# Score rows and turned states by way of DRAM in a four-layer graph network: one kernel, one change

## The chip, the cores and the metric

The kernel runs on one core of a Trainium2 chip. A core has TensorE (PE) for matrix products, VectorE (DVE), ScalarE (ACT) and GpSimd (POOL) for elementwise work, SyncE (SP), which here only issues transfers, and 16 DMA engines. Matrix products end in PSUM, eight banks of 128 x 512 float32; everything else lives in SBUF (128 partitions) or in DRAM. Each engine works through its own instructions in order and waits for others by semaphores.

The metric is the device time of one execution in microseconds, as the median of three runs: 2783.21 us before the change (2779.62 to 2784.21). About 0.2% (5.6 us) can be told from no change.

## The reference

There are 128 graphs of 128 nodes with 256 features and an adjacency matrix. Four layers follow one another, each with a residual and a normalisation:

```python
x = layernorm(x + L0(x, adj))   # attention, 4 heads of 64
x = layernorm(x + L1(x, adj))   # 3 steps of a gated recurrent unit (GRU)
x = layernorm(x + L2(x, adj))   # relations: one masked sum and product each
x = layernorm(x + L3(x, adj))   # attention, 1 head
```

In an attention layer the score of a pair of nodes is the sum of a row term and a column term:

```python
e = leaky_relu(e_src[:, :, None, :] + e_dst[:, None, :, :], 0.2)
e = where(adj > 0, e, -inf);  alpha = softmax(e, axis=2)
out = elu(einsum('bijh,bjhf->bihf', alpha, Wh))
```

The second term has to lie along the row of the score matrix, the same on all 128 partitions: a column that a product left across partitions must be turned into a row and repeated. In the GRU layer each of three steps does this:

```python
m = h @ weight[i];  aggr = A^T @ m
gi = aggr @ w_ih.T + b_ih;  gh = h @ w_hh.T + b_hh
r = sigmoid(i_r + h_r);  z = sigmoid(i_z + h_z)
n = tanh(i_n + r * h_n);  h = (1 - z) * n + z * h
```

## The kernel before

**Groups and stages.** The graphs go in 33 groups: one of two graphs, 31 of four, one of two. For each group there are stages, written as Python generators; each `yield` ends one step of a stage. The stages are `loads` (l), `head` (h, layer 0), `tail` (t, layers 2 and 3), two lanes of gate products `reset_and_new` and `new_and_update` (p and q), and two lanes for the elementwise part of the GRU, `chunk_0` and `chunk_1` (u and v), one for each half of the 256 features.

**The written order.** Strings of letters say which stage of which group takes its next step. START fills the pipeline, STEPS is one turn of a loop in steady state (31 turns, one for each group of four), END drains it. In a turn, different groups are in different stages. A last pass ties all instructions of an engine to the order in which they were written, so an engine never overtakes: what stands behind a waiting instruction waits too. All transfers of the steady state go through SP's one queue.

**Gates** (L585). The 256 x 256 products of the GRU use Strassen's scheme: seven products instead of eight for each gate and source, with sums of blocks formed by POOL (state) and DVE (aggregate) in `right_sums` (L553, operation at L560). A gate holds a pair of PSUM banks, "sums" (chunk 0) and "gate" (chunk 1), until ACT and DVE have read it. ACT copies at L607 and L609 and DVE additions at L617 and L625 stand between its products (L597). `GATES, OTHERS = 2, 4`: two such pairs, and four banks in turn for everything else ("ps").

**A GRU step** (`chunk`, L637). For each half, ACT makes r, n and z, DVE makes the new state `hT` (L669, L670), features along partitions. For the next step the state is also needed with nodes along partitions: four PE transposes into a ps bank (L679), copied by ACT to `hN` (L683). Then `neighbours` (L571) multiplies it by the adjacency, ACT copies the aggregate (L580), and DVE forms its block sums.

**Score rows** (`as_rows`, L404). DVE splits the column terms into three bf16 parts, which together hold the float32 value (L412 to L415); PE transposes them (L419), ACT copies the rows out (L422). A matmul with a column of ones at the three right places (`picks`) then repeats a row over all partitions (L478 in the head, L800 in the tail), and DVE adds the other term and the mask out of PSUM (L482, L803), giving `em`.

**By way of DRAM.** Four other transpositions already use no PE: `to_dram` (L300) stores a tile, `from_dram` and `squares` (L310, L130) read it back with four DMAs that put 32 x 32 squares in each other's places, and DVE transposes inside the squares (L333, L519, L719, L823). For the first or last group (`by_pe`) PE does it instead.

Of the kernel before, what the change touches and what calls it, by code (L numbers as in the profile page):

```python
# [16 lines left out]
P = 128  # L17
N = 128
# [7 lines left out]
GATES, OTHERS = 2, 4  # L26
# [20 lines left out]
IN_TURN = [("p", 14), ("q", 10), ("u", 3), ("v", 3), ("p", 10), ("q", 14), ("u", 11), ("v", 13)]  # L47
# [4 lines left out]
FIRST = {"a": ("c", 0), "b": ("h", 0), "c": ("l", 0), "d": ("f", 0), "e": ("l", 1), "f": ("h", 1), "g": ("l", 2), "h": ("u", 0), "i": ("v", 0), "j": ("p", 0), "k": ("q", 0), "l": ("h", 2), "m": ("u", 1), "n": ("v", 1), "o": ("t", 0), "p": ("p", 1), "q": ("q", 1)}  # L52
START = """
aaababababcbbbbbcbdbbabbedbbbbdddbdddddddddddddddbbdaabbfddddbbbbbbbbbbbdbbbbbefdddddfbdbbbdbcbddbbd
ddbdffbbbbbffffbdffbcgghfiiijhhhkifijjjjfkjjjfijffjakkkjjkjhfkkkjijjfjjjkheijjjjkkkfkkkkkijkhffffhkk
kfhihhhkhfkhhjiiijkffiiiihfffklhhiijjiikkkijjjjjkjajllkkkjjjkiffflijjhkjhkfjjjkkkffjjjkkkkkhkhhjiihk
khhfffikfiihfliihhhhfjfiihfkkklffffkkiiijjiijjjjjjjkfkkjkfhjjjkaiiljjjkkkjjjkjjlhkhjkkhjdfkkgffhhikk
kikfmnkhliimmhmiiolppplddddpdnnpnqdddddddddddddd
"""
PERIOD = {"a": ("q", 0), "b": ("v", 0), "c": ("t", -2), "d": ("p", 0), "e": ("h", 1), "f": ("u", 0), "g": ("t", -1), "h": ("t", -3), "i": ("l", 2), "j": ("l", -1), "k": ("l", 0), "l": ("h", 2), "m": ("u", 1), "n": ("p", 1), "o": ("v", 1), "p": ("q", 1), "q": ("t", 0)}  # L60
STEPS = """
abcaddddaeaebdedfeedaedaaedabeabfbddfgaacdddeaaddgdafafedhaaeacdgfageaggfbabcaaefficfddbbggaggajeeea
fgggfgfebfgggggggdebbbkaadbblcdbgibbdddacdadacccgdlggcladeeedeelafdebgdbggadaafccccedacdadaaafaddbac
dafdeaffadebafffbdeefegbbdalbfeegefgabbgebfafdbbbeddgaadcbdddeedggeebddaaaefddefbaagbbgddaaeacdadafg
daadiaaaddfdaaaffedgfgllblbfgabbllemmlgnnmggogoonmnbponq
"""
LAST = {"a": ("q", -1), "b": ("l", -2), "c": ("p", -1), "d": ("v", -1), "e": ("t", -3), "f": ("t", -2), "g": ("u", -1), "h": ("t", -4), "i": ("l", -1), "j": ("t", -1)}
END = """
abacaaacaaddacceccfcgccedcahcdcgdccaccaaaaagcaaafggfeefcgaaagffggceefffffeffggaffagddddfffccgddgadcc
ddfaacdafadfcefccaaadffccadfffecaccgcdcggcdaaccccdaaaccgcggaaaaacaaddagdadggggdecaagdfcaafgdaagddcdf  # L70
dccffcdccdeeecfffcfcecfcfaaacfffaeidgdcaeffcgaaacccaafcjaaccgdggagccafjadddafgeaaigddfejjejjjjejjjjj
jjjjffffjjjjjjjffffjjjfffjjjjfjjjjffjjjjjfjjjfffjjjjjjjjjjjjjjjjjjjjjjj
# [8 lines left out]
def kernel(ctx: ExitStack, tc: tile.TileContext, a: dict, out: bass.AP):  # L81
# [88 lines left out]
    def state(g):  # L170
        by_pe = {"head": g == 0, "tail": g == NG - 1}
        return {"g": g, "graphs": spans[g], "n": sizes[g], "relations": 1, "by_pe": by_pe, **layers()}
# [15 lines left out]
    for l, tag in enumerate(("x3T_0", "o", "x3_0")):  # L188
# [34 lines left out]
    identb = cp.tile([P, P], BF16, tag="identb", name="identb")  # L223
    picks = {}
# [4 lines left out]
    def constants(st):  # L229
# [11 lines left out]

        nc.vector.tensor_copy(identb, ident)
        yield
        for T in (G * H, G):
            one = ring(sp, [3 * T, T], F32, "pick", f"one_{T}", 2)
            nc.vector.tensor_add(one, ident[: 3 * T, :T], ident[: 3 * T, T : 2 * T])
            nc.vector.tensor_add(one, one, ident[: 3 * T, 2 * T : 3 * T])
            picks[T] = cp.tile([3 * T, T], BF16, tag=f"pick{T}", name=f"pick_{T}")
            nc.vector.tensor_copy(picks[T], one)
            yield  # L250
# [153 lines left out]
    def as_rows(st, cols, name):  # L404

        n, h = cols.shape[1], cols.shape[2]
        full = ring(sp, [P, 3, G, h], BF16, "split", f"split_{name}", 2)
        if n < G:
            nc.vector.memset(full, 0.0)
        t = full[:, :, :n]  # L410
        r = ring(sp, [P, n, h], F32, "rest", f"rest_{name}", 2)
        nc.vector.tensor_copy(t[:, 0], cols)  # L412
        nc.vector.tensor_sub(r, cols, t[:, 0])
        nc.vector.tensor_copy(t[:, 1], r)
        nc.vector.tensor_sub(t[:, 2], r, t[:, 1])  # L415
        yield
        k = 3 * G * h
        ps = ring(pp, [P, 1024], BF16, "ps", "psb", OTHERS)[:k, :N]
        nc.tensor.transpose(ps, full.rearrange("p k g h -> p (k g h)"), identb)  # L419
        yield  # L420
        st["rows"] = ring(sp, [k, N], BF16, "rows", f"rows_{name}", 2)
        nc.scalar.copy(st["rows"], ps)  # L422
        yield
# [7 lines left out]
    def head(st):  # L431
# [20 lines left out]
        wh = sp.tile([P, n, D + 2 * H], F32, tag="wh0", name=f"wh0_{g0}")  # L452
        for g in range(G):
            if g < n:
                ps = bank(D + 2 * H)
                for c in range(C):
                    matmul(ps, xT[:, c, ts(g, N)], w0[:, c, :], start=c == 0, stop=c == C - 1)
            yield
            if g < n:
                nc.scalar.copy(wh[:, g, :], ps)  # L460
            yield
# [477 lines left out]
```

## Time and profile before

| | us |
|---|---|
| median of three runs | 2783.21 |
| span of the profiled execution | 2778.8 |
| idle time of PE before 138 us | 31.6 |
| idle time of PE after 2622 us | 35.5 |
| one turn of the loop in steady state | 82.8 |

The runs take 0.8 to 5.4 us more than the span, which counts from the first to the last instruction of the profiled execution; no other time of that execution is given. The profile tells busy time by engine, the chain of work that ended last, groups of instructions by source line, and transfers. A product in float32 is recorded as two instructions; a transpose as one. PE's pieces in the chain give the pace at which it moves on, which is shorter than the duration of one instruction, because instructions overlap.

In the table of groups each row has the line, the engine, the operation, what it writes and reads, how often, and then the busy time, the mean of one in nanoseconds, and the idle time before it with what ended that. Four rows for an idea of sizes:

```profile
L580 ACT COPY agT<-ps 128x512 f32<-128x512 f32 (+1 forms) x198 | 112.6, 569 | 100.0 <-PE ps L115 100.0
L482 DVE SCALAR_TENSOR_TENSOR em<-ps,wh,nbias 128x128 f32<-128x128 f32 x512 | 140.6, 339 | 37.3 <-PE ps L115 37.3
L669 DVE SCALAR_TENSOR_TENSOR d<-z,d 128x512 f32<-128x512 f32 (+1 forms) x198 | 147.1, 743 | 15.0 <-ACT h2N L683 10.3
L607 ACT COPY sums<-gate 128x256 f32<-128x256 f32 (+1 forms) x396 | 141.6, 358 | 140.6 <-PE gate L597 138.1
```

### The profile page before, as it was taken

The page shows a single profiled execution, that of the slowest core. Times are in us where ns is not written, and L with a number is a line of the kernel's source. Part 1 is how long each engine was busy: PE and PEld are TensorE (multiplying, and loading weights), DVE is VectorE, ACT ScalarE, POOL GpSimd, SP SyncE. Part 2 cuts the span into 40 slices and gives each one's busy share as a digit, 9 for nine tenths or more (in the row PEclk, how much of TensorE's full clock was granted, in tenths as well). Part 3 has the DMA queues.
Part 4 walks back from the last instruction along what each step waited for, and adds up shares of the span by engine and source line. Part 5 has one row for each costly group of instructions (what it writes and reads, how often), then busy time and mean ns, then how long its engine had stood idle before and what let it go on. Part 6 is the DMA issues. An engine that isn't in the chain of part 4 may idle for free.

```text
span 2778.8 us, 44698 instructions
## 1 busy us (share of the span) xinstructions
PE 2702.2 (97%) x14490; PEld 2293.2 (83%) x14490; DVE 2208.4 (79%) x5269; ACT 1781.0 (64%) x4570; POOL 913.2 (33%) x925
## 2 busy tenths in 40 slices
PE   6899999999999999999999999999999999999986
PEld 4788888888888888888888888888888888888874
DVE  6677887878888878888877888887888787888765
ACT  3556766666666666666666666666766666666645
POOL 0223333324333323333323333323333333333331
PEclk9999999999999999999999999999999999999997
DMA  3344455444555444545444545445446545445321
GB/s 101 68 83 95 90 112 111 86 93 92 108 102 113 85 92 97 108 96 118 89 88 98 103 95 118 95 88 97 98 95 118 101 88 100 93 97 107 80 51 47
DMA packets 1177038, 263.73 MB, mean 95 GB/s; under 512 B 929888, under 2 KB 1176544, under 8 KB 1176800
## 3 DMA queue, kind: packets, MB, share of 16 engines
q1 hardware_dynamic: 1172272, 257.00, 46.0%
q10 hardware_dynamic: 4528, 3.81, 0.5%
q8 instruction: 118, 1.93, 0.3%
q14 instruction: 120, 0.98, 0.1%
HBM read 153.10 MB, written 107.61 MB: 94 GB/s over the span
## 4 chain that ended last, share of the span: by engine, by line
PE 93%; DVE 4%; ACT 1%; DMA 1%; issue 0%; POOL 0%; SPq 0%; ACTq 0%; POOLq 0%; DVEq 0%
PE gate L597 44%; PE ps L115 29%; PE sums L597 18%; PE ps L118 2%; DVE em L482 1%; DVE gate L625 1%; ACT em L397 0%; PE psb L419 0%; DMA vec<-in_L_gnn_a_dst_dram 0%; DMA factors_h<-in_L_gnn_w_hh_dram 0%; DVE d L669 0%; DVE em L393 0%; DVE nm L394 0%; DVE sums L617 0%; DVE st_x L347 0%
## 5 line engine op out<-in xcount | busy, mean ns | idle before, releaser
L597 PE MATMUL gate<-T_h,factors_h 128*128 128x256 f32 (+1 forms) x2376 | 691.5, 379 | 10.1 <-DVE gate L625 8.6
L597 PE MATMUL gate<-T_a,factors 128*128 128x256 f32 (+1 forms) x2376 | 677.3, 373 | 2.2 <-DVE T_a L560 2.0
L597 PEld LDWEIGHTS gate<-T_h,factors_h 128*128 128x128 f32 x2376 | 424.5, 190 | 93.3 <-DVE gate L625 27.6
L597 PEld LDWEIGHTS gate<-T_a,factors 128*128 128x128 f32 x2376 | 443.9, 191 | 59.2 <-DVE T_a L560 2.5
L597 PE MATMUL sums<-agT,factors 128*128 128x256 f32 (+1 forms) x1188 | 347.5, 374 | 2.2 <-ACT sums L607 1.0
L661 ACT ACTIVATE n<-n,bih 128x512 f32<-128x512 f32 (+1 forms) x198 | 140.5, 709 | 264.7 <-DVE n L659 264.7
L397 ACT ACTIVATE em<-em,nm 128x128 f32<-128x128 f32 x640 | 247.9, 391 | 6.3 <-DVE nm L394 6.2
L597 PEld LDWEIGHTS sums<-agT,factors 128*128 128x128 f32 x1188 | 220.5, 190 | 35.9 <-DVE sums L617 1.6
L664 POOL TENSOR_TENSOR d<-h2T,n 128x512 f32<-128x512 f32 (+1 forms) x66 | 82.2, 1245 | 466.9 <-ACT n L661 466.9
L607 ACT COPY sums<-gate 128x256 f32<-128x256 f32 (+1 forms) x396 | 141.6, 358 | 140.6 <-PE gate L597 138.1
L722 POOL TENSOR_TENSOR x<-x,x 128x512 f32<-128x512 f32 x63 | 78.8, 1272 | 458.2 <-DVE x L719 444.7
L360 ACT ACTIVATE x<-x,mr_x,rs_x 128x256 f32<-128x256 f32 x384 | 198.7, 589 | 11.2 <-DVE mr_x L355 11.2
L115 PE MATMUL ps<-wh,aT 128*128 128x64 f32 (+1 forms) x1280 | 188.5, 295 | 1.3 <-PE gate L597 0.6
L597 PE MATMUL gate<-agT,factors 128*128 128x256 f32 (+1 forms) x594 | 178.6, 382 | 2.4 <-ACT r L649 2.4
L115 PEld LDWEIGHTS ps<-wh,aT 128*128 128x128 f32 x1280 | 169.1, 192 | 12.9 <-PE gate L597 1.5
L580 ACT COPY agT<-ps 128x512 f32<-128x512 f32 (+1 forms) x198 | 112.6, 569 | 100.0 <-PE ps L115 100.0
L353 POOL TENSOR_TENSOR rs_x<-rs_x,neghalf 128x4 f32<-128x4 f32 (+1 forms) x99 | 98.8, 998 | 232.1 <-DVE rs_x L352 232.1
L657 DVE SCALAR_TENSOR_TENSOR n<-r,n 128x512 f32<-128x512 f32 (+1 forms) x198 | 127.0, 668 | 58.0 <-ACT n L655 58.0
L482 DVE SCALAR_TENSOR_TENSOR em<-ps,wh,nbias 128x128 f32<-128x128 f32 x512 | 140.6, 339 | 37.3 <-PE ps L115 37.3
L669 DVE SCALAR_TENSOR_TENSOR d<-z,d 128x512 f32<-128x512 f32 (+1 forms) x198 | 147.1, 743 | 15.0 <-ACT h2N L683 10.3
L353 POOL TENSOR_TENSOR rs_o<-rs_o,neghalf 128x4 f32<-128x4 f32 (+1 forms) x33 | 43.4, 1314 | 349.9 <-DVE rs_o L352 343.7
L752 POOL TENSOR_TENSOR x<-x,b 128x256 f32<-128x256 f32 x128 | 133.1, 1068 | 52.2 <-ACT h1N L683 45.0
(170 smaller groups left out, 6123.0 us busy)
## 6 DMA issues: line engine op xcount, KB each, us to landing
d_em<-em SPq DMA_DIRECT2D x63, 512.0 KB, 3.4
aT<-d_em SPq DMA_DIRECT2D x252, 128.0 KB, 3.7
x0s<-in_x_dram SPq DMA_DIRECT2D x248, 64.0 KB, 2.6
adj<-in_adj_dram SPq DMA_DIRECT2D x62, 256.0 KB, 3.3
x<-in_x_dram SPq DMA_DIRECT2D x31, 512.0 KB, 4.8
d_h0T<-x SPq DMA_DIRECT2D x62, 256.0 KB, 3.0
h0T<-d_h0T SPq DMA_DIRECT2D x124, 128.0 KB, 3.8
d_h<-h3T SPq DMA_DIRECT2D x62, 256.0 KB, 2.3
```

The costliest lines, as they stand in the source:

```text
L115: nc.tensor.matmul(ps, lhsT, rhs, start=start, stop=stop)
L353: nc.gpsimd.tensor_tensor(rs, rs, neghalf[:, :n], ALU.pow)
L360: nc.scalar.activation(y[:, g, :], y[:, g, :], AF.Identity, bias=mr[:, g : g + 1], scale=rs[:, g : g + 1])
L397: nc.scalar.activation(em[:, r, :], em[:, r, :], AF.Exp, bias=nm[:, i : i + 1], accum_out=den[:, i : i + 1])
L482: nc.vector.scalar_tensor_tensor(em[:, g - k, h, :], rows_of[g][:, h, :], wh[:, g, D + h : D + h + 1], nbias[:, g, :], ALU.add, ALU.add,)
L580: nc.scalar.copy(t, ps)
L597: nc.tensor.matmul(into, w[:, SEL[name], k - 1], layer[source][k], start=start, stop=True, skip_group_check=True)
L607: nc.scalar.copy(c11, c21)
L657: nc.vector.scalar_tensor_tensor(n, tr, 1.0, n, ALU.add, ALU.mult)
L661: nc.scalar.activation(n, n, AF.Tanh, bias=bih[:, 2 * C + c : 2 * C + c + 1])
L669: nc.vector.scalar_tensor_tensor(d, tz, 1.0, d, ALU.add, ALU.mult)
L752: nc.gpsimd.tensor_add(x2[:, g, :], x2[:, g, :], b2)
```

## The change

Four things change together.

1. Score rows: `as_rows` and the constants `identb` and `picks` go. Each graph's column terms (in the tail: all graphs' at once) are stored to DRAM as rows, one float at a time, by `to_rows`, and read back by `from_rows` with the row repeated over all partitions, straight into `em`. DVE then adds the other term and the mask in place.
2. New states: for all groups but the first and the last (`gru` in `by_pe`) the state `hT` is stored to DRAM as it is, read back in four DMAs of squares into `hN`, and transposed inside the squares by DVE.
3. PSUM: three pairs of gate banks and two other banks.
4. START, STEPS and END are written anew. The loop runs 29 turns; START and END hold the rest. In a turn, steps of the next group's GRU and those of the present one's last step stand side by side. The tile `o` gets a second buffer, DRAM tiles get rings of their own, and `x1` and `edge` are looked up when they are used.

```diff
-GATES, OTHERS = 2, 4
+GATES, OTHERS = 3, 2
...
-PERIOD = {"a": ("q", 0), "b": ("v", 0), "c": ("t", -2), "d": ("p", 0), "e": ("h", 1), "f": ("u", 0), "g": ("t", -1), "h": ("t", -3), "i": ("l", 2), "j": ("l", -1), "k": ("l", 0), "l": ("h", 2), "m": ("u", 1), "n": ("p", 1), "o": ("v", 1), "p": ("q", 1), "q": ("t", 0)}
+PERIOD = {"a": ("v", -1), "b": ("p", 0), "c": ("q", 0), "d": ("h", 1), "e": ("v", 0), "f": ("u", 0), "g": ("t", -1), "h": ("t", -2), "i": ("l", 2), "j": ("l", -1), "k": ("h", 2), "l": ("t", -3), "m": ("u", 1), "n": ("v", 1), "o": ("p", 1)}
 STEPS = """
...
+abcbcbccdecbfcccghbbcbfcebgcdhcbebibfbeccdgbcbccdcfgjcbcfbdfgceegcighfehdcfcehggbgcfghfccgedeegfbgde
+gdgkccglgdfdcegffcgjcefgebcbehcbdgedcbbdebgbhcbghlhcgcchdbfbdgcbcgbdehbbbhfkcckdbdbcfcbebfbbcfbgdfe
+ecegfdcfbdkgdeecfgcekeggddbdefecggdecgcgdckgdfgccdcfckdgfcdcdbfebhebecdelbgcbcbbcgcibdgebbhcbcdcdbfk
+emmkbblbkbbgkfnbfmcbfbcenbmfbofeefknncooeeocfkoeonoog
 """
...
-        by_pe = {"head": g == 0, "tail": g == NG - 1}
+        by_pe = {"head": g == 0, "gru": g in (0, NG - 1), "tail": g == NG - 1}
...
-    def as_rows(st, cols, name):
...
+    def to_rows(cols, name):
+
+        d = ring(dp, [cols.shape[1], N], F32, "rows", f"d_rows_{name}", 10)
+        nc.sync.dma_start(d.rearrange("r m -> m r"), cols)
+        return d
+
+    def from_rows(t, rows):
+
+        nc.sync.dma_start(t, rows.rearrange("r m -> (r m)").partition_broadcast(P))
...
@@ head
                 nc.scalar.copy(wh[:, g, :], ps)
-            yield
-        yield from as_rows(st, wh[:, :, D + H :], f"0_{g0}")
-        rows = st["rows"]
+                rows[g] = to_rows(wh[:, g, D + H :], f"0_{g0}_{g}")
+            yield
...
             for g in range(k, k + 2):
-                ps = rows_of[g] = bank(H, N)
-                for h in range(H):
-                    i = g * H + h
-                    matmul(ps[:, h, :], picks[G * H][:, i : i + 1].to_broadcast([3 * G * H, P]), rows)
-                yield
+                from_rows(em[:, g - k].rearrange("p h m -> p (h m)"), rows[g])
+            yield
             for g in range(k, k + 2):
                 for h in range(H):
                     nc.vector.scalar_tensor_tensor(
                         em[:, g - k, h, :],
-                        rows_of[g][:, h, :],
+                        em[:, g - k, h, :],
...
@@ chunk
             if l + 1 < L:
 
-                ps = bank(G, N)
-                for g in range(G):
-                    transpose(ps[:, g, :], hT[:, ts(g, N)])
+                by_pe = st["by_pe"]["gru"]
+                if not by_pe:
+                    d = ring(dp, [G * P, P], F32, "turnh", f"d_h{l + 1}{c}_{g0}", 4)
+                    nc.sync.dma_start(d.rearrange("(g p) m -> p g m", p=P), hT.rearrange("p (g m) -> p g m", g=G))
                 yield
                 yield from right_sums(nc.gpsimd, hT, st["layers"][l + 1]["h"], c, f"h{l + 1}_{g0}")
                 hN = ring(sp, [P, G, N], F32, "hN", f"h{l + 1}N{c}_{g0}", 2)
-                nc.scalar.copy(hN, ps)
-                yield
-                yield from neighbours(hN, edge, st["layers"][l + 1]["a"], c, f"{l + 1}_{g0}")
+                flat = hN.rearrange("p g m -> p (g m)")
+                if by_pe:
+                    ps = bank(G, N)
+                    for g in range(G):
+                        transpose(ps[:, g, :], hT[:, ts(g, N)])
+                else:
+                    from_dram(flat, d)
+                yield
+                if by_pe:
+                    nc.scalar.copy(hN, ps)
+                else:
+                    nc.vector.transpose(flat, flat)
+                yield
+                yield from neighbours(hN, st["edge"], st["layers"][l + 1]["a"], c, f"{l + 1}_{g0}")
...
@@ tail
-        yield from as_rows(st, wh[:, :, D + 1 :], f"3_{g0}")
+        rows = to_rows(wh[:, :, D + 1], f"3_{g0}")
+        yield
...
-        ps = bank(n, N)
-        for g in range(n):
-            matmul(ps[:, g, :], picks[G][:, g : g + 1].to_broadcast([3 * G, P]), st["rows"])
+        from_rows(em.rearrange("p g m -> p (g m)"), rows)
...
-    for p in range(1, NG - 1):
+    for p in range(2, NG - 2):
```

## The prediction

> **What bounds the kernel now.** I read the page's busy shares first, then one turn of the loop (82.8 us, four graphs) by stretches, then the chain of waits inside that turn, then the queues.
>
> ```profile
> PE 2702.2 (97%) x14490; PEld 2293.2 (83%) x14490; DVE 2208.4 (79%) x5269; ACT 1781.0 (64%) x4570; POOL 913.2 (33%) x925
> ...
> PE 93%; DVE 4%; ACT 1%; DMA 1%; issue 0%; POOL 0%; SPq 0%; ACTq 0%; POOLq 0%; DVEq 0%
> ```
>
> ```profile
> 1048.30:1131.10 82.80, 82.64 (x445) 70.54 (x444) 68.02 (x161) 55.05 (x141) 28.52 (x28) 1.00 0.49 99
> ```
>
> The single row is the stretch of one turn: length, then busy PE, PEld, DVE, ACT, POOL, granted clock, DMA share. TensorE is full, at clock 1.00, and the chain runs through it for 93%. Busy PE is pipelined, so I price PE work by the chain, whose pieces are the pace at which PE moves on. These pieces of the same turn (start, length, what) are those the change touches:
>
> ```profile
> 1054.91 0.44 PE ps L118 x4
> ...
> 1077.54 0.44 PE ps L118 x4
> ...
> 1081.47 0.44 PE ps L118 x4
> ...
> 1100.96 0.15 PE psb L419
> ...
> 1112.33 0.17 PE psb L419
> ...
> 1113.56 0.55 PE ps L115 x8
> ...
> 1115.20 0.43 DVE gate L625
> 1115.64 1.02 DVE em L482 x4
> 1116.66 0.35 DVE gate L625
> ...
> 1124.47 0.33 PE ps L115 x4
> ...
> 1128.48 0.33 PE ps L115 x4
> 1128.81 0.59 PE ps L118 x4
> ```
>
> L118 are the transposes of new states, L419 the transposed scores, the short L115 pieces the rows laid out by matmul. The DVE pieces are the only real stop of PE in the turn, 1.80 us: L625 stands behind the score additions.
>
> **What goes.** Transposes 0.44+0.44+0.44+0.59 = 1.91 us. Head rows 0.55+0.33+0.33 = 1.21; the tail's four row matmuls start at 1103.02 and PE goes on at 1103.34, so 0.32. L419: 0.15+0.17 = 0.32. Together 3.76 us per turn, all on the path. ACT loses four copies to hN (595 ns) and two to rows (256): 2.9 us, off the path. DVE loses eight split operations of about 0.17 us, 1.4. A floor for a turn without any stop is 82.8 - 3.76 - 1.8 = 77.2 us. Removing the constants (identb, picks) touches only the start, where PE waits for weights; I cost it at nothing.
>
> **What comes, per turn.**
> DVE: four transposes 128x512, the L823 row's 690 ns: 2.8 us. The score additions read SBUF instead of PSUM; L659 has 684 and 672 ns from PSUM where L669 and L670 have 690 to 770 from SBUF, so no change. DVE: 68.0 - 1.4 + 2.8 = 69.4 us. In a turn of 79 that is 88%, against 82% now: not the bound, but each wait of DVE for a transfer now reaches the gate additions (L617, L625) behind it sooner.
>
> SP, which issues everything in order: four stores of states, 16 reads, five stores of score columns, five broadcasts, 30 DMAs beside 49. The reads of d_h take 0.56 us each on SP, stores 0.38 to 0.47: 9.0 + 1.7 + about 4.5 = 15 us, onto 34 us of issues in SP's timeline of this turn. 49 of 79 us: it fits, but each read also waits at the queue's head for its store to land.
>
> DMA engines: 0.487 x 82.8 x 16 = 645 engine-us for 37,254 packets, 17.3 ns each. Added packets: 2048 of 512 B, 8192 of 128 B, 2560 of one float, 640 of 2 KB: 13,440, at the same mean 233 engine-us. (645+233)/16 = 55 us, 69% of 79. Not the bound.
>
> **The new wait: hT by way of DRAM.** Now a turned state costs 0.44 us PE and 0.6 us ACT. Then:
>
> ```profile
> d_h<-h3T SPq DMA_DIRECT2D x62, 256.0 KB, 2.3
> ...
> aT<-d_em SPq DMA_DIRECT2D x124, 64.0 KB, 2.7
> ```
>
> The store has the size of the first row (2.3 us to landing; the like d_h0T takes 3.0). Each of the four reads has the size of the second; the last is issued 1.7 us after the first (0.56 each). With the transpose: 2.3 to 3.1 + 1.7 + 2.7 + 0.69 = 7.4 to 8.2 us from state to edge product. What hides it is PE work written in between. I set each step's instructions beside its letter in the new STEPS and added the PE steps at the pace of the chain (0.43 us for a gate product, 0.88 for an edge product, 1.73 for a w2 pair). Between the state's step and its edge product stand 9.6 and 7.3 us (chunks 0 and 1, first layer) and 9.6 and 8.7 (second layer). On SP chunk 0's reads are written behind chunk 1's store, so they wait for chunk 1's state: 0.4 + 1.7 + 2.7 + 0.69 = 5.5 us, against 5.6 and 5.7 written. So only chunk 1 of the first layer is short, by 0.1 to 0.9 us; I take 0.5. If the cover were gone, each turned state would cost 6.4 to 7.2 us more than now.
>
> **Score rows.** The broadcasts' nearest row is the 256 KB adj load, 3.3 us. A column store writes single floats to DRAM, which no row shows. By number of packets it equals a load of adjacency squares (512 packets, 2.4 to 4.1 us). Against it speaks the Trainium skill, "DMA: Bandwidth & Descriptors": Rules for kernel authors say a strided last dimension becomes one descriptor per element and should be avoided; its Specifications say that below 512 B the engine reads, modifies and writes. If those writes ran one after another at the 0.2 us HBM access of its Latency section, 32 per engine make 6.4 us. The tail's store is written 5.7 us of PE before the additions that use it: by the row 2.6 + 3.3 = 5.9, short by 0.2; by the rule 9.7, short by 4.0 in each turn. Nothing here runs such a write; I take the row, since packets cost 17.3 ns whatever their size, and keep 0 to 4.0. The head's first two columns have 17 us and more of cover; its broadcast is written 3.0 us ahead of its addition, so DVE may wait 0.3 us, which PE need not see.
>
> **Three gate pairs, two other banks.** PE now refills a ps bank after two uses, not four. By the same count the emptying copy or addition is written 0.4 to 1.7 us ahead of the refill in ten places and level with it in one; copies take 0.37 to 0.84. I put 0.8 us per turn on it, 0 to 2. The third gate pair lets r, nh and z of the next layer start sooner: that is the cover above, not a further gain. The DVE stop of 1.8 us: L482 stays, its matmuls go; I leave 0.6. Stops after: 0.5 + 0.2 + 0.8 + 0.6 = 2.1 us.
>
> A second rule against the change: "VectorE: DVE Perf Modes", Rules for kernel authors, has a 128x128 transpose go to TensorE where PSUM will do. By the chain it costs the full engine 0.11 us each; by DVE, an engine with 14.8 us free, 0.17. By the rule the 1.91 us stay and the gain is 59 us smaller; I take the row, because here TensorE sets the turn.
>
> **The sum.** A turn: 77.2 + 2.1 = 79.3, 3.5 less. Over 31 full groups 109 us. The ends (before 138 us and after 2622 us PE is idle 31.6 + 35.5 us by the stretches) are written anew; I leave their idle time, 20 us either way. The span 2778.8 lies 4.4 below the median 2783.2; the difference is taken off the median: **2674 us**.
>
> **Rivals.**
> Covered, as forecast: 0.60, 2615 to 2735 (stops 0.8 to 4.0, ends 20).
> Partly covered: stops of 4 to 5.4, since landings stretch when 30 more DMAs share the queue: about 2755; 0.11. For: the DMA share is up to nine tenths in slices of the turn. Against: the written distances.
> Slower: **SP's single queue makes the turn of states the bound.** The reads of d_h landed in up to 4.7 us. If stores and reads both do so, the chain is 4.7 + 1.7 + 4.7 + 0.69 = 11.8, short by 4.5 in the first layer and 3.1 in the second: stops 7.6 + 1.6 = 9.2, a turn of 86.4, 2895 us. It decides from a chain of 10.0 us on (2 x 10.0 - 7.3 - 8.7 = 4.0, with 1.6 the 5.6 that go). For: DVE at 88% and SP both serve in order. Against: medians of 2.3 to 3.3. Chance 0.25; slow single-float writes end here too.
> Better: no stop but 0.5 us and shorter ends, about 2610; 0.04.
> A measurement tells about 0.2%, 5.6 us, from no change. Faster 0.71, same 0.04 (the edge of the partly covered case), slower 0.25. The range leaves out most of the slower case: 2605 to 2815.
>
> **What would show it.** Right: a turn near 79 us, PE still over 90% of the chain, hN transposes waiting under 1 us for DMA, DVE near 69 us, DMA share near 0.69. Wrong: DVE or PE at the head of the chain waiting for hN or em transfers; column stores landing in over 5 us; SP waiting on its own stores; PE waiting for ps evacuations beyond 2 us a turn.

## The result and the profile after

The changed kernel takes 3866.53 us (median of 4 runs, 3865.49 to 3867.05) against 2782.1 us for the old one beside it: 1.390 times as long, with a 95% interval of 1.388 to 1.392. The forecast was 2674 us, and the range to 2815 us does not hold it. The sign was wrong as well.

The head of the page of the kernel after: span, busy time by engine, the granted clock in 40 slices, and SP's queue.

```profile
span 3863.4 us, 44097 instructions
...
PE 2935.0 (76%) x13290; PEld 2449.9 (63%) x13290; DVE 2396.5 (62%) x5118; ACT 1711.7 (44%) x4380; POOL 877.4 (23%) x925
...
PEclk8889898888888888888888898988888888888987
...
q1 hardware_dynamic: 1607312, 364.34, 64.4%
```

PE has 1200 instructions fewer than before (13290 against 14490), as the change says, but is busy 233 us longer (2935.0 against 2702.2), and for 24% of the span it does nothing. The row of the clock says why fewer instructions take longer: 0.8 to 0.9 of full speed in nearly every slice, 0.862 on average, where before it was 0.993. A wait costs twice here: once for the idle time, and again for the slow pace behind it, as a stretch below shows.

One turn is now 117.3 us (703.5 us over six turns between the first loads of `x0s` of a group), against 82.8. The stretch of most of one turn after, with the same columns as in the prediction:

```profile
1904.30:2020.40 116.10, 90.56 (x406) 76.17 (x405) 74.13 (x156) 52.88 (x134) 27.23 (x28) 0.85 0.69 100
```

Before, a turn had 82.64 us of busy PE in it; less the 3.76 us removed that would be 78.9. Here it is 90.56: 11.7 us more, which is the clock, and 25.5 us in which PE is idle. The DMA share of 0.69 is the number that was forecast, but of a longer turn: 0.69 of 116.1 is 80 us of the engines' time, where 0.69 of 79 was 55. The engines are not full, and still have far more to do than was counted.

What DVE and PE wait for, from the page's groups: busy time and mean, then the idle time before the group and what ended it.

```profile
L463 DVE SCALAR_TENSOR_TENSOR em<-em,wh,nbias 128x128 f32<-128x128 f32 x512 | 244.2, 541 | 226.9 <-DMA em<-d_rows 226.8
...
L123 PE MATMUL ps<-edge,h2N 128*128 128x128 f32 x512 | 99.6, 356 | 210.6 <-DVE h2N L676 210.5
```

The score additions (before L482, now L463) wait for the broadcast of the rows, and the edge product for the turned state. Both are DMA chains, so who holds them up? SP's own waits (line, tile and transfer waited for: us in total, times, longest):

```profile
SPq L408 <- DMA d_rows<-wh: 263.9, 36, 10.5
...
SPq L142 <- DMA d_h<-h2T: 239.3, 35, 9.2
```

The broadcast (L408) stands at the head of SP's queue until the store of the column terms has landed, and the reads of squares (L142) until the store of the state has. The second is a plain 256 KB store, whose like landed in 2.3 us before. One stretch of SP's timeline (start, length, line, transfer) shows it:

```profile
1958.60 0.38 SPq L661 DMA_DIRECT2D d_h<-h2T  x1
1960.73 0.38 SPq L403 DMA_DIRECT2D d_rows<-wh  x1
1961.66 0.36 SPq L661 DMA_DIRECT2D d_h<-h2T  x1
1962.11 12.70 SPq L142 DMA_DIRECT2D h2N<-d_h  x8
1974.91 0.98 SPq L403 DMA_DIRECT2D d_rows<-wh  x2
1983.29 0.34 SPq L408 DMA_DIRECT2D em<-d_rows  x1
```

From the first of the eight reads to the last it takes 12.70 us, where 0.56 each make 4.5. The last four are issued only at 1972.91, when the second store of a state has landed, 11 us after its issue. A store of single floats (1960.73) stands between the two state stores. PE in the same stretch:

```profile
1967.09 0.59 PE L578 MATMUL gate<-T_h,factors_h 128*128 128x256 f32 x2
1974.40 2.05 PE L123 MATMUL ps<-edge,h2N 128*128 128x128 f32 x8 [6.72 <-DVE h2N L676]
1976.24 1.06 PE L578 MATMUL gate<-T_h,factors_h 128*128 128x256 f32 x2
1977.10 1.06 PE L578 MATMUL gate<-h2T,factors_h 128*128 128x256 f32 x2
...
1981.77 0.59 PE L578 MATMUL sums<-h2T,factors_h 128*128 128x256 f32 x2
1982.20 0.59 PE L578 MATMUL gate<-T_a,factors 128*128 128x256 f32 x2
```

PE is idle for 6.72 us; behind it, pairs of a gate product start 0.86 us apart, and from 1981.77 on 0.43 apart. That is the clock: the granted clock of the six microseconds from 1974.40 is 0.50, of the six from 1981.77 it is 0.95. The trace agrees with what the Trainium skill, "TensorE: Matmul & The Clock Gate", Part 1, says of a clock that halves after an idle window and comes back only after sustained work; the page gives about 3.4 us for either, and here the slow pace lasted some 6.

The profile alone doesn't decide between two readings: that the stores of single floats are slow and take the rest with them, or that too many transfers in one queue make the states' way through DRAM late (the prediction's slower rival).

### The profile page after: what moved, and what is told of

Same layout as the page of the kernel before. It is cut to its first block, busy times and chain, and to the rows that moved or that the text cites. A ratio compares the mean times of both kernels' runs of the same rounds, so it can differ in the third digit from the quotient of the medians.

```text
span 3863.4 us, 44097 instructions
## 1 busy us (share of the span) xinstructions
PE 2935.0 (76%) x13290; PEld 2449.9 (63%) x13290; DVE 2396.5 (62%) x5118; ACT 1711.7 (44%) x4380; POOL 877.4 (23%) x925
## 3 DMA queue, kind: packets, MB, share of 16 engines
q1 hardware_dynamic: 1607312, 364.34, 64.4%
## 5 line engine op out<-in xcount | busy, mean ns | idle before, releaser
L578 PE MATMUL gate<-T_a,factors 128*128 128x256 f32 (+1 forms) x2376 | 731.4, 398 | 192.2 <-DVE T_a L541 190.7
L578 PE MATMUL gate<-T_h,factors_h 128*128 128x256 f32 (+1 forms) x2376 | 773.0, 415 | 45.5 <-DVE gate L606 34.7
L578 PEld LDWEIGHTS gate<-T_h,factors_h 128*128 128x128 f32 x2376 | 484.9, 215 | 143.3 <-DVE gate L606 33.9
L463 DVE SCALAR_TENSOR_TENSOR em<-em,wh,nbias 128x128 f32<-128x128 f32 x512 | 244.2, 541 | 226.9 <-DMA em<-d_rows 226.8
L578 PE MATMUL sums<-h2T,factors_h 128*128 128x256 f32 (+1 forms) x396 | 135.7, 428 | 207.0 <-DVE sums L598 204.4
L123 PE MATMUL ps<-edge,h2N 128*128 128x128 f32 x512 | 99.6, 356 | 210.6 <-DVE h2N L676 210.5
L123 PEld LDWEIGHTS ps<-edge,h2N 128*128 128x128 f32 x512 | 90.9, 260 | 226.7 <-issue 213.3
L578 PEld LDWEIGHTS sums<-h2T,factors_h 128*128 128x128 f32 x396 | 78.6, 210 | 230.7 <-DVE sums L598 218.0
L123 PE MATMUL ps<-edge,h1N 128*128 128x128 f32 x512 | 119.5, 409 | 132.4 <-issue 112.5
L123 PEld LDWEIGHTS ps<-edge,h1N 128*128 128x128 f32 x512 | 112.4, 313 | 149.5 <-issue 141.5
```

What stands on the lines that cost most here:

```text
L123: nc.tensor.matmul(ps, lhsT, rhs, start=start, stop=stop)
L463: nc.vector.scalar_tensor_tensor(em[:, g - k, h, :], em[:, g - k, h, :], wh[:, g, D + h : D + h + 1], nbias[:, g, :], ALU.add, ALU.add,)
L578: nc.tensor.matmul(into, w[:, SEL[name], k - 1], layer[source][k], start=start, stop=True, skip_group_check=True)
```

## The experiments

Times are given beside the old kernel's on the same chip, which was 2780.8 to 2784.5 us in all of them. "Turn" is worked out as above over six to nine turns. Runs without an interval are single ones; four runs of the last kernel below lie 12 us apart, so differences of that size between single runs say little.

### What makes the rows and states late

**The rows in the order in which they lie in SBUF.** Each partition stores its column terms side by side, 16 bytes in the head's and 8 to 16 in the tail's store.

```diff
-        d = ring(dp, [cols.shape[1], N], F32, "rows", f"d_rows_{name}", 10)
-        nc.sync.dma_start(d.rearrange("r m -> m r"), cols)
+        d = ring(dp, [N, cols.shape[1]], F32, "rows", f"d_rows_{name}", 10)
+        nc.sync.dma_start(d, cols)
...
-        rows = to_rows(wh[:, :, D + 1], f"3_{g0}")
+        rows = to_rows(wh[:, n - 1, D + 2 - n :], f"3_{g0}")
```

> The changed kernel, but the score columns are stored as they lie: each partition writes its four floats side by side (128 pieces of 16 B), and the broadcast reads the same 2 KB; the tail stores four neighbouring columns of one graph. The scores so laid out are permuted, so values differ from the reference's. Theory A (each store of single floats holds the DMA engines for about 8 us, and all that is queued behind it comes late): about 2700 us, 2640 to 2780. Theory B (turning the states by way of DRAM through SP's one queue is too slow): above 3500. Theory C (two other banks and the new order stall PE): above 3300.

3070.56 us, turn 91.7, clock 0.960. Three quarters of the loss go with 128 pieces in place of 512. None of the three forecasts holds: the stores are most of the loss, but not all of it.

**The states by VectorE alone.** No store and no reads of squares; DVE transposes `hT` within its squares straight into `hN`. The rows' stores stay.

```diff
-                    nc.sync.dma_start(d.rearrange("(g p) m -> p g m", p=P), hT.rearrange("p (g m) -> p g m", g=G))
...
-                    from_dram(flat, d)
...
-                    nc.vector.transpose(flat, flat)
+                    nc.vector.transpose(flat, hT)
```

> The changed kernel without the store and the reads of the states: VectorE transposes hT inside its squares straight into hN, and the squares are not put in each other's places, so values differ. The stores of single floats stay. Theory A: still far above before, 3100 to 3600, since the tail's additions and the stores of h0T and h3 still stand behind the single floats. Theory B: about 2700. Theory C: above 3500.

3701.67 us, turn 110.6, clock 0.883. With all 20 of the states' DMAs gone from a turn, 165 of 1084 us are regained. The states' way through DRAM is not the main cause. More is left than the 3100 to 3600 of theory A, and the number lies in the range of theory C; but C had also put the kernel with natural rows above 3300.

**The rows turned by DVE first.** The column terms are copied into a tile of 32 columns, DVE transposes its squares, and the store writes 128-byte pieces.

```diff
-        nc.sync.dma_start(d.rearrange("r m -> m r"), cols)
-        return d
...
+        nc.vector.tensor_copy(columns[k][:, :n], cols)
+        t = ring(sp, [P, Q], F32, "square", f"square_{name}", 4)
+        nc.vector.transpose(t, columns[k])
+        d = ring(dp, [Q, N], F32, "rows", f"d_rows_{name}", 10)
+        nc.sync.dma_start(d.rearrange("j (b m) -> b j m", m=Q), t)
+        return d[:n]
```

> The changed kernel with the rows made by VectorE: the columns are copied into a tile of 32, transposed in squares and stored in pieces of 128 B; the broadcast stays. Five copies and five transposes of 128x32 on VectorE a turn are added, about 1.6 us. Theory A: 2660 to 2800. Theories B and C: above 3300.

3108.59 us, turn 92.1, clock 0.954. This is the change with nothing left out and another store, and well above the 2660 to 2800 that the first theory gave it.

**The old kernel with the stores added.** The five stores of single floats in a turn are issued as in the new kernel; nobody reads them.

```diff
                 nc.scalar.copy(wh[:, g, :], ps)
+                to_rows(wh[:, g, D + H :], f"0_{g0}_{g}")
...
+        to_rows(wh[:, :, D + 1], f"3_{g0}")
```

> The kernel before with the stores of single floats added at the same places (five in a turn), read by nobody; all else stays. Theory A: slower by some hundreds of us, 2900 to 3500, because transfers of the old order queue behind them. Theories B and C: within 1% of before.

3255.0 us, turn 97.7, clock 0.931: 474 us, 14.9 a turn, for stores that no instruction waits for directly. Two rows of its waits (engine, tile, line, releaser: us, times, longest):

```profile
DVE h0T L333 <- DMA h0T<-d_h0T: 388.2, 32, 19.4
...
PE gate L603 <- DVE h0T L333: 332.5, 32, 17.5
```

The old kernel's own turned states `h0T` come up to 19.4 us late, and PE waits for them; between 600 and 2400 us of the old kernel alone DVE has no such wait. What stands behind such a store in the queue is late, whatever it is.

**Number or kind of pieces.** Two kernels keep the changed kernel's 512 pieces of a store and its broadcasts of 2 KB. In the first each piece is 64 bytes long; in the second it is one float, but the floats lie 64 bytes apart, in ten tiles that are zeroed once at the start (`spread`). Neither makes the right scores, because the broadcast reads only the first 2 KB; they serve to price the store.

```diff
-        d = ring(dp, [cols.shape[1], N], F32, "rows", f"d_rows_{name}", 10)
-        nc.sync.dma_start(d.rearrange("r m -> m r"), cols)
+        d = ring(dp, [G, N, 16], F32, "rows", f"d_rows_{name}", 10)
+        nc.sync.dma_start(d.rearrange("r m k -> m r k"), cols)
...
-                rows[g] = to_rows(wh[:, g, D + H :], f"0_{g0}_{g}")
+                rows[g] = to_rows(wh[:, g, :D].rearrange("p (r k) -> p r k", r=G)[:, :, :16], f"0_{g0}_{g}")
...
```

```diff
-        d = ring(dp, [cols.shape[1], N], F32, "rows", f"d_rows_{name}", 10)
-        nc.sync.dma_start(d.rearrange("r m -> m r"), cols)
...
+        d = spread[k][: cols.shape[1]]
+        nc.sync.dma_start(d.rearrange("r m k -> m r k")[:, :, :1], cols.unsqueeze(2))
```

> The changed kernel with as many pieces in each store as before (512, in the last group 512 too) but each of 64 B, taken from other columns of wh; the broadcast reads the first 2 KB of what was stored, so values differ. If the number of pieces that go to DRAM is what costs: as slow as the changed kernel, 3700 to 4100, and 9 us or more from the last store's issue to its read. If the small size of a piece is what costs: near the run with natural stores, 3000 to 3150, and 2 to 4 us.

3037.64 us, turn 90.5, clock 0.963.

> The changed kernel with single floats, as many as before, but each stored 64 B from the next, so that no two of them share 64 B of DRAM; the broadcast reads the first 2 KB of the zeroed and sparsely written tile, so values differ. If many writers of one piece of 64 B are what costs: 3000 to 3200, and 2 to 4 us from the last store to its read. If the float's size alone costs (a piece is read, changed and written back): 3700 to 4100, and about 9 us.

3029.84 us, turn 90.1, clock 0.965. The same number of stores, pieces and bytes as in the changed kernel, and 837 us less: only the places of the floats in DRAM differ. Neither the number of pieces nor their size is the price. SP's queue has the same 1607312 packets in both, and the page gives the time that they took, as a share of 16 engines (64.4% of 3863.4 us in the changed kernel, shown above):

```profile
q1 hardware_dynamic: 1607312, 364.34, 62.3%
```

Of 3027.4 us that is 602 us less for the same packets: 3.7 us of all 16 engines for each of the 161 stores.

The last group of each kernel gives the price of one store when the queue is nearly empty. Its tail stores two graphs' terms, and the broadcast behind it is issued as soon as that has landed. The changed kernel, SP's timeline:

```profile
3833.61 0.38 SPq L403 DMA_DIRECT2D d_rows<-wh  x1
...
3842.79 0.34 SPq L408 DMA_DIRECT2D em<-d_rows  x1
```

The kernel with floats 64 bytes apart:

```profile
3006.18 0.38 SPq L410 DMA_DIRECT2D spread<-wh  x1
3007.79 0.34 SPq L415 DMA_DIRECT2D em<-spread  x1
```

From start to start 9.18 us against 1.61, each for 256 floats. The same difference in the others:

| store of the last group | us | in other kernels |
|---|---|---|
| 256 single floats side by side | 9.18 | 9.23 |
| 128 pieces of 8 bytes side by side | 2.96 | 3.37 |
| 128 pieces of 128 bytes | 1.95 | 2.60 |
| 512 pieces of 64 bytes | 1.84 | none |
| 256 single floats, 64 bytes apart | 1.61 | 1.61 to 1.82 in seven |

### What is left: 90 us a turn, not 79

With the stores mended, the kernel is still 249 us slower than the old one (3029.84 against 2780.83). The stretch from 600 to 2400 us of the kernel with spread floats, with the columns of the prediction:

```profile
600.00:2400.00 1800.00, 1642.93 (x8051) 1386.62 (x8051) 1500.26 (x3103) 1046.99 (x2670) 549.19 (x555) 0.97 0.66 129
```

In each of these 20.0 turns PE is busy 82.1 us: 7.9 us of idle time and 3.2 us more than the 78.9 that should be left, at a clock of 0.97 there.

**The score additions with two operands in SBUF.** The old kernel, with one operand changed: the additions read `nbias` from SBUF in place of the row from PSUM.

```diff
-                        rows_of[g][:, h, :],
+                        nbias[:, g, :],
```

> The kernel before with one operand changed: the head's score additions read the mask from SBUF twice instead of the rows from PSUM, so the rows are left out of the scores; PE still makes them. Theory D (a VectorE operation with two operands in SBUF gives way to GpSimd, one from PSUM doesn't): the mean of these additions rises from 340 ns to 400 to 600, and the time by 20 to 120 us. Otherwise: 340 ns and no change, within 0.3%.

2811.52 us (4 runs, 2809.41 to 2813.56): 1.0109 times, interval 1.0092 to 1.0126. One line's instructions, in the old kernel (count, then least, median and greatest ns, then where in the span):

```profile
L482 DVE SCALAR_TENSOR_TENSOR em<-ps,wh,nbias x512: 331/340/352, 23.1 to 2607.9; 128x128 f32<-128x128 f32 x171
```

and in this one:

```profile
L482 DVE SCALAR_TENSOR_TENSOR em<-nbias,wh x512: 332/343/1369, 22.1 to 2641.0; 128x128 f32<-128x128 f32 x171
```

The least and the median agree, so the operation is no slower by itself; some take four times as long, and the mean goes from 339 to 431 ns. In the changed design they are stretched more. The group in the kernel with spread floats, 600 to 2400 us:

```profile
L470 DVE SCALAR_TENSOR_TENSOR em<-em,wh,nbias 128x128 f32<-128x128 f32 x320 | 175.7, 613 | 1.4 <-DMA em<-spread 1.3
```

**Without GpSimd's bias additions.** In the timeline of the kernel with natural rows, eight score additions took 5.53 us (from 1528.83) while GpSimd was at its state sums and then at four additions of the bias `b2`. So these four were left out of the kernel with spread floats.

```diff
-            for g in range(k, k + step):
-                nc.gpsimd.tensor_add(x2[:, g, :], x2[:, g, :], b2)
```

> The run with floats 64 B apart, without GpSimd's four additions of the bias in layer 2, so the bias is left out. Theory D (a VectorE operation with two SBUF operands stretches while GpSimd works): the head's score additions, 613 ns in the mean, fall to 400 to 520, PE's wait before the edge products falls from 4.6 us a turn to 1 to 3, the time by 50 to 130, to 2900 to 2980. Otherwise, since GpSimd is idle 70% of the time: no change beyond 15.

2953.17 us, turn 87.8, clock 0.978, 77 us less. The same group:

```profile
L470 DVE SCALAR_TENSOR_TENSOR em<-em,wh,nbias 128x128 f32<-128x128 f32 x320 | 136.4, 491 | 3.8 <-DMA em<-spread 3.8
```

These four additions made DVE slower by 122 ns in each of its 16 score additions a turn, 2.0 us together, and the turn is 2.3 us shorter without them. PE's wait before the edge products falls from 4.6 to 2.8 us a turn. A second way leads from these additions to PE, since DVE's L770, which empties a "ps" bank, uses their result; but the trace with the additions has DVE idle before L770 only for PE (14.0 us in all), never for GpSimd. The stretching is the rule of the Trainium skill, "SBUF — State Buffer", Who interferes with whom: a DVE instruction with two SBUF inputs contends with a GpSimd instruction that reads SBUF, while one with at most one SBUF input, outside the modes that use both ports, doesn't; by the page's Summary the later of the two waits until the first has finished. The trace agrees: 352 ns at most with a PSUM operand, 1369 with two from SBUF.

**The states' way again, with the stores out of the way.** The kernel with natural rows, with DVE turning the states as in the second experiment.

> The changed kernel with both: natural stores, and no transfers of the states (VectorE transposes hT inside its squares). Values differ. What the turn of states by way of DRAM costs once the single floats are gone: theory B says 200 us or more, so 2650 to 2850; theory D (the additions and GpSimd) says little of the rest goes, so 2950 to 3070; theory C (two other banks, the new order) says the same as D, with PE waiting for the emptying of banks.

3023.96 us, turn 89.8: 47 us less than with the way through DRAM. No transfer of the states is left, and PE still waits for them (us between 600 and 2400 us, times, longest):

```profile
PE ps L123 <- DVE h1N L671: 92.0, 20, 5.0
```

So this wait is for DVE, which comes late to the transpose, and not for a landing.

**Moving steps in the written order.** In the stretch between the first and the second GRU step, DVE's timeline of the kernel with natural rows has softmax work and the other transposes written ahead of the turned state, one right behind the other:

```profile
1528.83 5.53 DVE L463 SCALAR_TENSOR_TENSOR em<-em,wh,nbias 128x128 f32<-128x128 f32 x8
1534.39 1.23 DVE L389 SCALAR_TENSOR_TENSOR em<-em 128x1024 f32<-128x1024 f32 x1
1535.65 1.22 DVE L390 TENSOR_REDUCE nm<-em 128x8 f32<-128x1024 f32 x1
1536.79 1.23 DVE L429 STREAM_TRANSPOSE x0s<-x0s 128x1024 f32<-128x1024 f32 x1
...
1538.59 0.70 DVE L676 STREAM_TRANSPOSE h1N<-h1N 128x512 f32<-128x512 f32 x1
```

PE's wait ends 0.10 us after that last line does, though the profile names nothing that ended it ("issue"):

```profile
1531.25 3.62 PE L123 MATMUL ps<-w,hr 128*128 128x256 f32 x16
1539.39 1.84 PE L123 MATMUL ps<-edge,h1N 128*128 128x128 f32 x7 [4.53 <-issue]
```

So in the kernel with spread floats one letter of STEPS, the turn of the first state, was moved ahead of the softmax step:

```diff
-gdgkccglgdfdcegffc...
+gfdgkccglgddcegffc...
```

(At its end this line of STEPS reads `bbcfbfgdfe`; where the change is shown above, one f is missing there.)

> The run with floats 64 B apart, and one letter of STEPS moved: VectorE's transpose of chunk 0's new state (first layer) is written ahead of the softmax of the head's second half instead of behind it and behind the transpose of x0s, 3.7 us of VectorE earlier. If what PE waits for there (4.6 us a turn) is VectorE's queue: the wait falls below 2 us and the time by 70 to 160, to 2870 to 2960. If it is the landing of the reads (theory B): VectorE waits for the transfer instead, and the time stays within 30 of 3030.

3046.81 us, turn 91.4: 17 us more. What PE waits for there, 600 to 2400 us:

```profile
PE ps L123 <- DVE x L770: 98.0, 20, 6.1
```

98.0 us in 20 turns, about as long as what it replaced, now for the addition that empties a "ps" bank, of which there are two. Replaced were these waits of the kernel with spread floats, the second again without a name, together 91.9 us in 21 times:

```profile
PE ps L123 <- DVE h1N L683: 64.4, 14, 4.9
PE ps L123 <- issue: 27.5, 7, 4.5
```

The time lies in the range that was to mean a late landing, but the wait is not for that.

The other way round: softmax and the transposes of `x0` moved behind both the emptying and the state.

```diff
-gdgkccglgdfdcegffc...
+ggccglgfdkddcegffc...
```

> Floats 64 B apart; the head's second softmax and the transpose of x0s (3.7 us of VectorE) are written behind the addition that empties the PSUM bank and behind the state's transpose. If VectorE's written order with its slowed additions is what PE waits for: 2880 to 2970, and PE's wait before the edge products 1 to 2.5 us a turn. If the landing of the states is: 3000 to 3050.

3037.44 us, turn 89.9, again in the range that was written for a late landing, and again with another wait, now for the gates' block additions:

```profile
PE sums L585 <- DVE sums L605: 82.3, 60, 2.7
```

Three orders, three names for the wait, and 17 us between them, not much more than the runs of one kernel can differ.

**Combinations.** The early turn of the first order without the states' way through DRAM:

> The run with the letter moved, and the states' store and reads left out (VectorE transposes hT inside its squares; values differ). It shows what the way through DRAM costs when VectorE's queue no longer covers it. Theory B: 60 to 200 below the run with the letter moved. Otherwise: within 40 of it.

3008.17 us, turn 89.3: 39 us less than that order with it. The early turn without the bias additions:

> The letter moved and GpSimd's bias additions left out, floats 64 B apart. If both act on the same wait: little below the better of the two alone (within 40). If on different ones: the sum of both, 2780 to 2880.

3041.46 us, turn 90.9: 88 us more than without the move, which neither forecast allowed. PE waits as before for the addition that empties a bank (98.5 us in 20 turns), and the turn of the state now comes before its data:

```profile
DVE h1N L683 <- DMA h1N<-d_h: 45.6, 20, 3.4
```

The later softmax without the bias additions:

> As the run with the softmax later, and without GpSimd's bias additions. If GpSimd's hold on VectorE adds to the order: 40 to 90 below that run. If the order alone mattered, or if the landing takes the place: within 20 of it.

3020.04 us, turn 89.3: 17 us for what gave 77 in the first order. And without the states' way as well:

> As the run before it, and without the states' store and reads (VectorE transposes hT inside its squares; values differ). What lies between the two is the cost of the states' way through DRAM, uncovered. Theory B: 60 to 200. Otherwise: 0 to 50, so that what is left above the forecast of 2674 lies in the order and VectorE's load.

2968.39 us, turn 88.1: another 52 us, between the two forecasts. DVE is still busy 73.4 us a turn (1500.97 over 20.4), and PE still waits 68.9 us in 20 turns for L605.

**The best complete version tried in this order.** Rows turned by DVE first, with the later softmax:

> Rows by VectorE's squares (as in the earlier run at 3109) with the softmax later; nothing left out. If the order's part carries over: 2960 to 3040. It adds two small VectorE operations for each store, which wait for ACT's copies; where these hold VectorE up: 3080 to 3110.

3103.5 us (4 runs, 3095.6 to 3107.46): 1.116 times the old kernel, interval 1.114 to 1.118. Against 3108.59 with the softmax where it was, that is no clear gain. No version that keeps the change came near the old time.

## Why the prediction was wrong

**The step that failed.** "By number of packets it equals a load of adjacency squares (512 packets, 2.4 to 4.1 us) ... I take the row, since packets cost 17.3 ns whatever their size, and keep 0 to 4.0." The 2.6 us were priced by a count, and the count is not what costs: 512 pieces of 64 bytes land within 1.84 us, 256 floats side by side take 9.18, and the same number 64 bytes apart 1.61. The "nearest row" had been chosen by a property that doesn't set the price. The other end of the bracket was too low too. Read-modify-write at 0.2 us each, 32 in a row on each engine, was to give 6.4 us for 512 floats; by that sum the last group's 256 would take 3.2, and they took 9.18. Over the whole kernel the 602 us of the engines' time make 118 ns for each of the 81920 floats, on top of what the same floats cost where they lie apart. The rule that speaks against a strided last dimension ("DMA: Bandwidth & Descriptors", Rules for kernel authors) gave the right direction, but with its reason, a descriptor per element, the spread floats would be as slow.

**What the sum left out.** Even at 9 us the prediction had one place for the price: the tail, where the row's user waits. It never asked what stands *behind* the stores. The kernel with stores that nobody reads answers that: 14.9 us a turn, three for each store. In the changed kernel the turned states and the broadcasts share the queue with five of them a turn. From the changed kernel to the one with spread floats a turn falls from 117.3 to 90.1 us; times 29 turns that is 789 of the 837 us.

**"The score additions read SBUF instead of PSUM; ... so no change."** Wrong, as the second cause, and the trace before could have told. The "690 to 770" leaves out one row of the same turn, and its timeline shows GpSimd at the bias additions around the longer of the two:

```profile
L670 DVE SCALAR_TENSOR_TENSOR h1T<-d,n 128x512 f32<-128x512 f32 x2 | 1.8, 896 | 0.1
...
1049.61 4.27 POOL L752 TENSOR_TENSOR x<-x,b 128x256 f32<-128x256 f32 x4 [1.49 <-ACT h1N L683]
...
1052.18 1.10 DVE L670 SCALAR_TENSOR_TENSOR h1T<-d,n 128x512 f32<-128x512 f32 x1
```

With both operands in SBUF it took 1.10 us there and 0.69 the other time; L659, with one from PSUM, never took more than 0.69 in the whole kernel. In the old kernel alone the operand costs 1.1%, and in the new design the mean is 613 ns. That is (613 - 339) x 16 = 4.4 us a turn, most of the miss of DVE's sum: 75.0 us (1500.26 over 20.0 turns) where 69.4 were forecast. That DVE would be "not the bound, but each wait of DVE for a transfer now reaches the gate additions (L617, L625) behind it sooner" was right in kind for L617 (now L605): there PE's wait ends up, though behind DVE's own work and not behind a transfer.

**The floor of 77.2** was too low. The 1.80 us called "the only real stop of PE in the turn" are pieces of the chain that run through DVE, and PE worked beside them (its timeline before):

```profile
1115.43 1.03 PE L597 MATMUL gate<-T_h,factors_h 128*128 128x256 f32 x4
1116.30 0.59 PE L597 MATMUL gate<-T_a,factors 128*128 128x256 f32 x2
1117.05 0.70 PE L597 MATMUL gate<-T_h,factors_h 128*128 128x256 f32 x2 [0.16 <-DVE gate L625]
```

PE stood still for 0.16 us, as its 82.64 busy us of 82.80 say too. The floor is 78.9, and with the other stops as forecast (0.5, 0.2 and 0.8) a turn is 80.4, not 79.3: some 34 us less gain. That is small beside the miss.

**The stops after**, 2.1 us by the forecast, are 11.2 above that floor in the kernel with spread floats (90.1 less 78.9): 7.9 us of idle time and 3.2 of slower pace. The distances had been counted in PE's instructions alone, as if DVE, busy for 83% of the turn there (75.0 of 90.1), stood ready at the end of each. Moving a step in the order only renamed the wait. And no price was put on the slow pace behind a gap: the old kernel's turn, at clock 1.00, has no gap to show it.

**The broadcast**, 3.3 us by the 256 KB load, landed in 4.8 (median) in the kernel with natural rows. With spread floats the head's additions wait for it 1.3 us and the tail's 10.1 us in 20 turns, 0.6 a turn in all where 0.2 was forecast for the tail: nearly covered.

**What was right.** PE lost the instructions that were to go. The states' way through DRAM, with its 20 transfers a turn on SP, is not the bound: it costs 39 to 52 us where the stores are mended (0.5 us a turn, 16 us in all, were forecast). So the rival on the slow side, SP's single queue, was not the cause, although its sign was the result's: with the states' transfers gone and the stores left, 920 us of the loss remain (3701.67 less 2782.1). In its last sentence ("slow single-float writes end here too") the real cause had been put away at a price of at most 4 us. The DMA share of 0.69 was met by luck: the engines' time and the turn were both half as long again as forecast. With spread floats it is 0.66 of 90.1, 59 us against 55.

**What stays open.** The kernel with the later softmax, no bias additions and no states' way has a turn of 88.1 us, still 8.8 above the forecast's 79.3. How much of that is the order planned with DVE times that don't hold, and how much the two "ps" banks, was not settled; two banks against four were not tried alone, because three gate pairs take the space. Why leaving out the bias additions gives 77 us in one order and 17 in another was not settled either. And of the slow stores the runs show when they are slow, not where in the chip the time goes. Nor was it tried to issue them from another queue than SP's, so whether they hold up only their own queue or every transfer on the 16 engines is not shown.

## What to carry to other kernels

Price an operation that no trace shows by measuring it alone, one variable at a time, before a sum rests on it; if that can't be done, ask what stands behind it in its queue, and not only who reads its result. Don't let many partitions write single elements side by side into DRAM: turn them on chip first, or leave space between them (the second was only priced here, with a broadcast that doesn't gather the floats). And on an engine that is over four fifths busy and works in order, an operand that moves from PSUM to SBUF is not free while GpSimd works, and a step that moves a little earlier may only give the wait another name. When rows of a profile are compared, take all rows of the kind: the one left out was the one that told.

## What the runs showed of the hardware

- The price of a store to DRAM depends on how close its pieces lie: 9.18 us for 256 floats side by side, 2.96 and 3.37 for 128 pieces of 8 bytes, 1.6 to 2.6 from 64 bytes on, whether as long pieces or as distance. Where between 8 and 64 bytes it changes wasn't tried with an empty queue; the 2 KB stores of 16-byte pieces in the kernel with natural rows landed in 2.0 us (median), those of spread floats in 2.1.
- For the same number of packets, 512 floats side by side took 3.7 us more of all 16 engines than 512 floats 64 bytes apart.
- Such a store delays transfers that have nothing to do with it: waits of up to 19.4 us for a read of squares.
- GpSimd stretches DVE's operations with two SBUF operands from a median of 343 to as much as 1369 ns in the same kernel, and those with one operand in PSUM not beyond 352.
- After a gap of 6.72 us PE's granted clock was 0.50 for about 6 us: 0.86 us a pair, then 0.43.
